# A four-layer convolution network in float32: second convolution's weights by accumulating transfers, shared rows copied, longer statistics pieces, one ScalarE reordering in the next chunk

## The chip, the core and the metric

The kernel runs on one core of a Trainium2 chip. A core has TensorE (PE, matrix products into PSUM), VectorE (DVE), ScalarE (ACT), GpSimd (POOL) and SyncE (SP), which work side by side, each in the order of its own queue, and wait for each other through semaphores. PEld is TensorE's loading of the stationary operand. Transfers are issued by SP, ACT or POOL and carried out by DMA engines. The metric is device time of one launch in microseconds (us); lower is better.

## The reference

The input `x` is (4, 256, 56, 56) in float32. Four layers follow each other, each `x = x + f(norm(x))`, where `norm` is a group norm over 8 channels and all positions. Layers 0 and 2 are involutions (a 7 x 7 kernel for each position, computed from the data), layer 3 gates by channel and position. The change lies in layer 1:

```
h = conv3x3(n, w1);  h = relu(bn1(h))        # n = norm(x)
h = conv3x3(h, w2);  h = bn2(h)
x = x + relu(n + h)
```

Each convolution has 256 channels in and out and a border of one zero.

## The kernel before, in words

`conv_layer` computes layer 1. Along a row, a 3-tap convolution is done for four outputs at a time with six products instead of twelve. A row of 56 becomes `WT` = 14 groups; `transform` makes six planes of the input (`v`, from the rows sorted into four phases, `ph1` or `ph2`); each of six planes of weights is multiplied with its plane on PE; and sums of the six results give the four outputs. The planes of weights from the three taps w0, w1, w2 of a row are: plane 0 6 w0, plane 1 w0 + w1 + w2, plane 2 w0 - w1 + w2, plane 3 w0 + 2 w1 + 4 w2, plane 4 w0 - 2 w1 + 4 w2, plane 5 24 w2. `row_weights` (L1236) makes them on DVE, for both convolutions, and `edge_weights` (L1265) scales planes 0 and 5 on ACT. PE takes the planes in the order 1, 2, 3, 4, 0, 5.

Channels lie on the 128 partitions, in two halves (`ci` of the input, `co` of the output). An image's rows are cut into three chunks, `C1_ROWS` for the first and `C2_ROWS` for the second convolution, so there are 12 chunks of each: (1, i) and (2, i). They are done in the order (1,0), (1,1), (2,0), (1,2), (2,1) and so on to (2,11): the second convolution runs one chunk behind. From chunk (1,1) on, the first convolution also saves products between pairs of rows (`columns`, `column_weights`, `filter_weights`), so a plane takes four products into two PSUM pairs, `inner` and `outer`; the second one (`unfiltered`) takes six products per half. PSUM holds four pairs, and a pair is reused when it has been read.

The order of all work is written out by hand. Each chunk has twelve slots, `after[0]` to `after[11]`; slot 2n runs inside the n-th plane of PE's order and slot 2n + 1 after its results were read. Other work is put there as small steps: loads, `phases` (L1322: the norm, and the sorting into phases, on ACT), `transform` (L1341, DVE) for the next chunk, and the weights at the start. `in_order` (L246) then ties each engine's instructions into program order, so a step that waits holds up all behind it on its engine.

At the end of a second convolution's chunk (`conv2`, L1506), `residual` (L1519, ACT) puts the normed input in `res`, `joined` (L1530, DVE) adds the convolution, ACT writes its relu in image order over the tile of x (L1542), and POOL issues a transfer that adds the layer's input to it (L1543) and one that stores it (L1544). `stats` (L1546) then sums pieces of 4 rows on DVE for layer 2's norm, in the next chunk's slots.

For layer 2, ten of these pieces of the last chunk are summed after the convolution has ended. Of the first convolution's chunk, the two outer output phases are written to `ph2` by `outputs` (L1432, ACT) in the next chunk, from the list `tail1`.

Of the kernel before, what the change touches and what calls it, by code (L numbers as in the profile page):

```python
# [56 lines left out]
C2_ROWS = [(0, 16), (16, 36), (36, 56)]  # L57
ST_ROWS = 4

# [12 lines left out]
def net_kernel(  # L72
# [1109 lines left out]
    def conv_layer(xin, xout, st, ahead):  # L1182
        with ExitStack() as es:
# [51 lines left out]

            def row_weights(u, wc, raw=None):  # L1236

                ws = []
                for ci in range(NB):
                    w = wc[ci * P : (ci + 1) * P].rearrange("c (y x) n -> c y x n", y=3)  # L1240
                    nc.sync.dma_start(u[:, ci, :, 0, :], w[:, :, 0, :])
                    nc.sync.dma_start(u[:, ci, :, 5, :], w[:, :, 2, :])
                    us = [u[:, ci, :, k, :] for k in range(WPOS)]
                    if raw is None:
                        w1 = new_xr()[:, : 3 * C].rearrange("p (y n) -> p y n", y=3)
                        nc.scalar.dma_start(w1, w[:, :, 1, :])
                        ws.append((us[0], w1, us[5], *us[1:5]))
                    else:
                        r = raw[ci][:, : 9 * C].rearrange("p (y x n) -> p x y n", y=3, x=3)
                        ws.append((r[:, 0], r[:, 1], r[:, 2], *us[1:5]))  # L1250
                yield
                for w0, w1, w2, u1, u2, u3, u4 in ws:
                    tt(u2, w0, w2, ALU.add)
                    tt(u1, u2, w1, ALU.add)
                    yield
                for w0, w1, w2, u1, u2, u3, u4 in ws:
                    tt(u2, u2, w1, ALU.subtract)
                yield
                for w0, w1, w2, u1, u2, u3, u4 in ws:
                    stt(u4, w2, 4.0, w0, ALU.mult, ALU.add)  # L1260
                    stt(u3, w1, 2.0, u4, ALU.mult, ALU.add)
                    stt(u4, w1, -2.0, u4, ALU.mult, ALU.add)
                    yield

            def edge_weights(u, ci):  # L1265

                for k, by in ((0, 6.0), (5, 24.0)):
                    nc.scalar.mul(u[:, ci, :, k, :], u[:, ci, :, k, :], by)

# [6 lines left out]
            def column_weights(ci, k0, k1):  # L1276

                w0, w1, w2 = (u1_sb[:, ci, y, k0:k1, :] for y in range(3))
                x = between_weights(ci, k0, k1)
                s = y_tile(3)[:, : (k1 - k0) * C].rearrange("p (k n) -> p k n", n=C)  # L1280
                tt(s, w0, w2, ALU.add)
                tt(x, s, w1, ALU.subtract)
                tt(w1, s, w1, ALU.add)
# [38 lines left out]
            def phases(i):  # L1322

                y0, y1, lo, hi = rows1(i)
                n, r0 = y1 - y0 + 2, lo - (y0 - 1)
                rstd, shift = norms[1][i // 3]
                if y0 == 0:
                    nc.vector.memset(ph1[:, :, 0], 0.0)
                if y1 == H:
                    nc.vector.memset(ph1[:, :, n - 1], 0.0)  # L1330
                for ci in range(NB):
                    at = ci * (CV_ROWS + 2) * W
                    xr = room["rows"][:, at : at + (hi - lo) * W].rearrange("p (r t j) -> p j r t", t=WT, j=4)
                    for j in range(4):
                        q, t0 = (j + 1) % 4, (j + 1) // 4
                        dst = ph1[:, PL[q], r0 : r0 + hi - lo, ci, t0 : t0 + WT]
                        s, t = rstd[:, ci : ci + 1], shift[:, ci : ci + 1]
                        nc.scalar.activation(dst, xr[:, j], AF.Identity, bias=t, scale=s)  # L1338
                        yield

            def transform(v, ph, y0, n):  # L1341

                rows = ph[:, :, y0 : y0 + n].rearrange("p j r c t -> p j (r c) t")
                at, size = rows[:, 0:1], ph.shape[2] * NB * (WT + 1)
# [33 lines left out]

            def new_v(key):
                v_of[key] = work.tile([P, WPOS, (CV_ROWS + 2) * NB, WT], F32, name="v")  # L1380
                return v_of[key]

            def input1(i):
                y0, y1, _, _ = rows1(i)
                n = y1 - y0 + 2
                yield from transform(new_v((1, i)), ph1, 0, n)

            def input2(i):
                y0, y1 = C2_ROWS[i % 3]
                yield from transform(new_v((2, i)), ph2, y0, y1 - y0 + 2)  # L1390

# [32 lines left out]
            def conv1(i, after, tail):  # L1424
# [4 lines left out]
                a, t, b, s, q = (y_tile(k)[:, : NB * n * WT] for k in (0, 1, 2, 5, 4))  # L1429
                home = {1: q, 2: s, 3: t, 4: s, 0: s}  # L1430

# [14 lines left out]
                for n_s, k in enumerate(KS):  # L1446
# [41 lines left out]
                    if k == 2:  # L1488
                        tt(full(a), full(q), got, ALU.add)
                        tt(full(q), got, full(q), ALU.subtract)  # L1490
                    elif k == 4:
# [14 lines left out]
            def conv2(i, after, sums, tail):  # L1506
# [23 lines left out]
                def joined(co):  # L1530
# [7 lines left out]
                    if i == n_chunks - 1:  # L1538
                        stt(xj, rj, 0.0, xj, ALU.max, ALU.add)
                        nc.sync.dma_start(xout[bb][co][:, at], x)  # L1540
                    else:
                        nc.scalar.activation(xj, rj, AF.Relu)  # L1542
                        nc.gpsimd.dma_start(x, xin[bb][co][:, at], accum_op=ALU.add)  # L1543
                        nc.gpsimd.dma_start(xout[bb][co][:, at], x)  # L1544

                def stats(co, ks):  # L1546

                    x = xr_of[i, co]
                    for k in ks:
                        at = (k * ST_ROWS - y0) * W  # L1550
                        nc.vector.bn_stats(sums[co][:, k, :], x[:, at : at + ST_ROWS * W])

# [36 lines left out]

                ks = list(range(y0 // ST_ROWS, y1 // ST_ROWS))  # L1590
                tail += [lambda co=co, part=part: stats(co, part) for co in range(NB) for part in (ks[:2], ks[2:])]


# [10 lines left out]
            order.append((2, n_chunks - 1))  # L1604
            late_v = None
            sums_of = {}


            since = mark()
            weights1, weights2 = row_weights(u1_sb, wc1, (room["h"], room["v2"])), row_weights(u2_sb, wc2)  # L1610
            next(weights1)
# [24 lines left out]
            for s, (conv, i) in enumerate(order):  # L1636
                after = [[] for _ in range(12)]
                for g in slow:
                    after[5].append(step(g))
                    after[11].append(step(g))  # L1640
                nxt = order[s + 1] if s + 1 < len(order) else None
                if conv == 1:
                    run_all(tail1)

                    if nxt[0] == 2:
                        j = nxt[1]
                        late_v = input2(j)
                        place(after, late_v, (1, 1, 3, 5, 8, 10))
                        if j == 0:
                            place(after, weights2, (3, 5, 7, 9, 11))  # L1650
                            for ci in range(NB):
# [6 lines left out]
                    else:  # L1658
                        j = nxt[1]
                        place(after, phases(j), [k // 2 for k in range(8)])  # L1660
                        after[3].append(lambda: load_rows(j + 1, xin))
                        place(after, input1(j), [4 + k // 2 for k in range(9)])
                        for ci in range(NB):
                            after[2 + ci].append(lambda ci=ci: edge_weights(u1_sb, ci))
                            after[4 + ci].append(lambda ci=ci: column_weights(ci, 1, 3))
# [3 lines left out]
                        for ci in range(NB):  # L1669
                            after[9 + ci].append(lambda ci=ci: column_weights(ci, 3, 5))  # L1670
                            after[10 + ci].append(lambda ci=ci: filter_weights(ci, 3, 5))
                        after[11].append(step(weights2))
                    conv1(i, after, tail1)
                else:
                    if i % 3 == 0:
                        sums_of[i // 3] = [
                            new_sums(H // ST_ROWS, work, 4)
                            if i // 3 < B - 1
                            else small.tile([P, H // ST_ROWS, 6], F32, name=f"st_c{co}", bufs=1)
                            for co in range(NB)  # L1680
# [3 lines left out]
                    tail1 = []  # L1684
                    if i == 0:
                        for ci in range(NB):
                            after[ci].append(lambda ci=ci: edge_weights(u2_sb, ci))
                    if late_v is not None:
                        place(after, late_v, (0, 0, 1))
                        late_v = None  # L1690
                    stats_at, loads_at = ((1, 2, 3, 4), (2, 4)) if i < n_chunks - 1 else ((3, 4, 6, 7), (4, 7))
                    for at, f in zip(stats_at, tail2):
                        after[at].append(f)
                    tail2 = []
# [20 lines left out]

            return tail2, sums_of[B - 1]

# [77 lines left out]
```

## Time and profile before

| what | us |
|---|---|
| median of 3 runs (1783.44 to 1788.03) | 1786.61 |
| profiled execution | 1782.26 |
| its span on the core | 1780.5 |
| PE busy | 1690.9 |
| DVE busy | 1359.5 |
| ACT busy | 904.5 |
| POOL busy | 398.2 |
| convolution layer, from its first product with weights to the next layer's first | 520.6 to 1228.6 |

The profile records one execution. A busy share is an average over stages: in the involution layers other things limit PE than in the convolution layer, so the layer concerned is read by itself. Behind a row of a timeline, the idle time before it stands in brackets with the engine and instruction that ended it. Names of lines (L1420) are those of the kernel before.

### The profile page before, as it was taken

Reading aid. Unit: us, or ns where it says so; the run is one execution under the profiler, and the core shown is the slowest. Engines: PE = TensorE matmul, PEld = TensorE weight load, DVE = VectorE, ACT = ScalarE, POOL = GpSimd, SP = SyncE. Lnnn points to the kernel's source line nnn. Section 1 sums busy time; section 2 is a strip of 40 time slices with the busy share of each in tenths; the row PEclk is TensorE's granted clock in tenths of the full one; section 3 lists DMA queues with packets and bytes.
Section 4 is the critical chain, followed back from the end, with each engine's and each line's share of the span. In section 5 each row is a group of like instructions: output and inputs, shape, how many; then the busy total and the mean of one; then the engine's idle time right before and its main releaser. Section 6 shows DMA issues by size and latency. Waiting matters only on the chain.

```text
span 1780.5 us, 55917 instructions
## 1 busy us (share of the span) xinstructions
PE 1690.9 (95%) x24216; PEld 1495.0 (84%) x24216; DVE 1359.5 (76%) x2529; ACT 904.5 (51%) x1926; POOL 398.2 (22%) x591
## 2 busy tenths in 40 slices
PE   6999999999998999999999999998999999899898
PEld 4998988889977988898889888986988888788786
DVE  2677787767779988789878887865877687677675
ACT  2655556555544334342344334223767567567564
POOL 2224321333210000000100000001000553563572
PEclk9999999999989999999999999999999999999996
DMA  2345443634652133331333232233445666665653
GB/s 86 125 162 169 139 151 135 198 108 130 207 173 80 41 87 77 94 75 51 90 92 76 52 87 55 63 126 108 144 142 164 188 210 193 209 208 162 187 152 115
DMA packets 71075, 227.46 MB, mean 128 GB/s; under 512 B 13141, under 2 KB 20830, under 8 KB 67118
## 3 DMA queue, kind: packets, MB, share of 16 engines
q1 hardware_dynamic: 55038, 160.97, 28.7%
q0 software_dynamic: 13952, 60.87, 12.1%
q8 instruction: 191, 3.13, 0.7%
q10 hardware_dynamic: 1840, 2.05, 0.4%
q14 instruction: 54, 0.44, 0.1%
HBM read 88.00 MB, written 49.15 MB: 77 GB/s over the span
## 4 chain that ended last, share of the span: by engine, by line
PE 57%; DVE 25%; ACT 7%; issue 5%; DMA 4%; POOL 1%; SPq 1%; ACTq 0%; DVEq 0%; POOLq 0%
PE mm L1420 18%; PE ps L592 14%; PE ps L634 13%; DVE kt L610 5%; PE ps L406 3%; DMA xw<-xw 3%; PE mm L1458 3%; DVE un L654 3%; ACT xs L1542 2%; PE ps L468 2%; DVE res L1534 1%; ACT res L1522 1%; DVE xs L1399 1%; DVE v L1362 1%; DVE st L1104 1%
## 5 line engine op out<-in xcount | busy, mean ns | idle before, releaser
L1420 PE MATMUL mm<-v,u_sb 128*128 128x280 f32 (+2 forms) x2136 | 478.0, 385 | 2.2 <-DVE v L1374 2.2
L1420 PEld LDWEIGHTS mm<-v,u_sb 128*128 128x128 f32 x2136 | 404.4, 190 | 71.4 <-issue 3.3
L634 PE MATMUL ps<-kt,xw 126*32 126x48 f32 (+1 forms) x12544 | 379.3, 235 | 19.4 <-DMA xw<-xw 7.4
L634 PEld LDWEIGHTS ps<-kt,xw 126*32 126x32 f32 (+1 forms) x12544 | 341.5, 122 | 64.4 <-issue 40.6
L592 PE MATMUL ps<-hp,z_sb 64*126 64x133 f32 x6144 | 383.7, 279 | 9.7 <-DVE kt L610 4.2
L592 PEld LDWEIGHTS ps<-hp,z_sb 64*126 64x126 f32 x6144 | 364.3, 186 | 25.4 <-DVE kt L610 6.4
L610 DVE TENSOR_TENSOR kt<-ps,zb_sb 126x798 f32<-126x798 f32 x352 | 332.9, 980 | 60.1 <-PE ps L592 59.6
L603 ACT ACTIVATE kt<-ps,zb_sb 126x133 f32<-126x133 f32 x960 | 280.2, 441 | 108.2 <-PE ps L592 108.2
L1458 PE MATMUL mm<-xs,u_sb 128*128 128x126 f32 (+1 forms) x1320 | 167.3, 280 | 19.1 <-DVE hp L1473 16.1
L1458 PEld LDWEIGHTS mm<-xs,u_sb 128*128 128x128 f32 x1320 | 159.4, 194 | 22.5 <-ACT ph L1338 16.1
L654 DVE SCALAR_TENSOR_TENSOR un<-ps,s,un 128x240 f32<-128x240 f32 x224 | 102.4, 457 | 90.7 <-ACT un L649 86.7
L654 DVE SCALAR_TENSOR_TENSOR un<-ps,par_sb,un 128x240 f32<-128x240 f32 x224 | 97.6, 456 | 82.3 <-ACT un L647 78.3
L418 ACT COPY xw<-ps 126x896 f32<-126x896 f32 x112 | 101.3, 906 | 50.2 <-PE ps L406 27.4
L406 PE MATMUL ps<-ident_sb,strip_sb 128*126 128x128 f32 x784 | 113.8, 285 | 13.5 <-issue 9.8
L659 POOL TENSOR_TENSOR xs<-un,xs 128x240 f32<-128x240 f32 x112 | 72.1, 664 | 216.9 <-DVE un L654 216.9
L149 POOL TENSOR_TENSOR norm_sb<-norm_sb,mhalf 128x1 f32<-128x1 f32 x32 | 19.3, 605 | 446.5 <-DVE norm_sb L148 446.5
L1543 POOL DMA_DIRECT2D xs<-x x22 | 19.7, 897 | 435.3 <-ACT xs L1542 435.3
L647 ACT ACTIVATE un<-ps,par_sb 128x240 f32<-128x240 f32 x112 | 50.1, 448 | 119.5 <-PE ps L634 110.7
L1542 ACT ACTIVATE xs<-res 128x1120 f32<-128x1120 f32 (+1 forms) x22 | 45.8, 2083 | 125.3 <-DVE res L1534 125.3
L406 PEld LDWEIGHTS ps<-ident_sb,strip_sb 128*126 128x126 f32 x784 | 85.6, 142 | 26.0 <-issue 11.8
L649 ACT ACTIVATE un<-ps,bn_t,s 128x240 f32<-128x240 f32 x112 | 60.1, 538 | 87.0 <-PE ps L634 80.0
L1338 ACT ACTIVATE ph<-xs,norm_sb 128x294 f32<-128x294 f32 (+2 forms) x96 | 82.0, 898 | 9.2 <-DMA xs<-x 7.5
(258 smaller groups left out, 1885.2 us busy)
## 6 DMA issues: line engine op xcount, KB each, us to landing
xw<-xw SPq DMA_DIRECT2D x224, 252.0 KB
xw<-xw SPq DMA_DIRECT2D x224, 126.0 KB
xs<-x SPq DMA_DIRECT2D x24, 560.0 KB
x<-xs POOLq DMA_DIRECT2D x8, 1568.0 KB, 8.1
xs<-x SPq DMA_DIRECT2D x8, 1568.0 KB
xs<-in_x_dram SPq DMA_DIRECT2D x6, 1568.0 KB
x<-xs SPq DMA_DIRECT2D x6, 1568.0 KB
gx<-x POOLq DMA_DIRECT2D x42, 224.0 KB, 5.2
```

The lines of the kernel that those rows point to most:

```text
L406: nc.tensor.transpose(ps[:Q, k * P : (k + 1) * P], flat[:, k * Q : (k + 1) * Q], ident_sb)
L418: nc.scalar.copy(xw[:, :NSB, :], ps[:Q, : NSB * P].rearrange("q (n c) -> q n c", n=NSB))
L592: nc.tensor.matmul(ps[:Q, i, k * NT : (k + 1) * NT], z_sb[i * R : (i + 1) * R, cb * GB // 2 + gp, z0 : z0 + Q], hp[i * R : (i + 1) * R, py ...
L603: nc.scalar.activation(kt[:, g0 + i, pb, :, k], ps[:Q, i, k * NT : (k + 1) * NT], AF.Identity, bias=zb_sb[:, cb * GB + g0 + i, p0 + k : p0 ...
L610: nc.vector.tensor_tensor(kt[:, g0 : g0 + 2, pb], ps[:Q, :, : PB * NT].rearrange("q i (k t) -> q i t k", k=PB), zb_sb[:, cb * GB + g0 : cb ...
L634: nc.tensor.matmul(v[m * j : m * j + m, i, :, k * TP : (k + 1) * TP], xw[:, window(ty), m * j : m * j + m], kt[:, ng * j : ng * j + ng, :, ...
L654: nc.vector.scalar_tensor_tensor(part, o[e], s, part, ALU.mult, ALU.add)
L659: nc.gpsimd.tensor_tensor(dst, u, dst, ALU.add)
L1338: nc.scalar.activation(dst, xr[:, j], AF.Identity, bias=t, scale=s)
L1420: nc.tensor.matmul(ps, *position(u, v, ci, dy, k, co, n), start=(j == 0), stop=(j == NB * 3 - 1))
L1458: nc.tensor.matmul(ps[:, bank, co * m : (co + 1) * m], u[ci][:, co * P : (co + 1) * P], v2[:, e, : n // 2, ci * WT : (ci + 1) * WT], start ...
L1542: nc.scalar.activation(xj, rj, AF.Relu)
```

## The change

Five edits are made together.

1. `summed_weights` replaces `row_weights` for the second convolution. The taps are loaded straight into the planes, ACT scales what needs a factor, and POOL issues nine steps of two transfers (one for each half `ci`) which add further taps from HBM, or plane 5, to what stands in a plane. Its last step is the scaling of planes 0 and 5, which was at the start of chunk (2,0) before and is now in slot 11 of (1,1).
2. `phases` and `transform` leave out the first two rows of a chunk that is not an image's first. ACT copies them, in all six planes, from the chunk before (`nc.scalar.copy` in `transform`). The planes stand in two fixed tiles, `v0` and `v1`, instead of tiles that rotate; the first convolution uses `v1` (chunk 0: `v0`), the second `v0` (last chunk: `v1`).
3. `stats` sums pieces of up to 8 rows (`ST_ROWS`), so a chunk of 20 rows has pieces of 8, 8 and 4.
4. ACT's reordering (L1542) and POOL's two transfers of the second half become `added`, and for `co` = 1 run in slot 0 of the next chunk (`late_x`).
5. `outputs` at the end of chunk (1,0) moves into slot 0 of (1,1); plane 1's result of a chunk then goes to another buffer, `first`. `transform` for the second convolution has five steps, not six, in the first convolution's slots.

The diff, cut to its core:

```diff
-ST_ROWS = 4
+ST_ROWS = 8
+ST_PIECES = [-(-(y1 - y0) // ST_ROWS) for y0, y1 in C2_ROWS]
...
+            def summed_weights(u, wc):
+
+                cis = range(NB)
+                w = [wc[ci * P : (ci + 1) * P].rearrange("c (y x) n -> c x y n", y=3) for ci in cis]
+                us = [[u[:, ci, :, k, :] for k in range(WPOS)] for ci in cis]
+                w1 = [new_xr()[:, : 3 * C].rearrange("p (y n) -> p y n", y=3) for ci in cis]
+                for ci in cis:
+                    nc.sync.dma_start(w1[ci], w[ci][:, 1])
+                    nc.sync.dma_start(us[ci][5], w[ci][:, 2])
+                    for k in (0, 1, 3):
+                        nc.sync.dma_start(us[ci][k], w[ci][:, 0])
+                yield
+                for ci in cis:
+                    nc.scalar.mul(us[ci][2], w1[ci], -1.0)
+                    nc.scalar.mul(us[ci][4], w1[ci], -2.0)
+                    nc.scalar.mul(us[ci][5], us[ci][5], 4.0)
+                    yield
+                for k, x in ((1, 1), (2, 0), (1, 2), (2, 2), (3, 1), (4, 0), (3, 1), (4, None), (3, None)):
+                    for ci in cis:
+                        by = us[ci][5] if x is None else w[ci][:, x]
+                        nc.gpsimd.dma_start(us[ci][k], by, accum_op=ALU.add)
+                    yield
+                for ci in cis:
+                    for k in (0, 5):
+                        nc.scalar.mul(us[ci][k], us[ci][k], 6.0)
+                yield
...
-                n, r0 = y1 - y0 + 2, lo - (y0 - 1)
+                n, r0, known = y1 - y0 + 2, lo - (y0 - 1), 2 if i % 3 else 0
...
-                    xr = room["rows"][:, at : at + (hi - lo) * W].rearrange("p (r t j) -> p j r t", t=WT, j=4)
+                    xr = room["rows"][:, at + known * W : at + (hi - lo) * W].rearrange("p (r t j) -> p j r t", t=WT, j=4)
...
-            def transform(v, ph, y0, n):
-
+            def transform(v, ph, y0, n, known):
+
+                if known is not None:
+                    old, m = known
+                    nc.scalar.copy(
+                        v[:, :, : 2 * NB].rearrange("p k r t -> p k (r t)"),
+                        old[:, :, m * NB : (m + 2) * NB].rearrange("p k r t -> p k (r t)"),
+                    )
+                    v, y0, n = v[:, :, 2 * NB :], y0 + 2, n - 2
...
+            v_sb = [wpool.tile([P, WPOS, (CV_ROWS + 2) * NB, WT], F32, name=f"v{k}") for k in range(2)]
...
+                first = y_tile(3)[:, : NB * n * WT] if i else q
+                home = {1: first, 2: s, 3: t, 4: s, 0: s}
...
-                        nc.scalar.activation(xj, rj, AF.Relu)
-                        nc.gpsimd.dma_start(x, xin[bb][co][:, at], accum_op=ALU.add)
-                        nc.gpsimd.dma_start(xout[bb][co][:, at], x)
...
+                        late_x.append(lambda: added(x, xj, rj, co, at))
+                        if co == 0:
+                            run_all(late_x)
+
+                def added(x, xj, rj, co, at):
+
+                    nc.scalar.activation(xj, rj, AF.Relu)
+                    nc.gpsimd.dma_start(x, xin[bb][co][:, at], accum_op=ALU.add)
+                    nc.gpsimd.dma_start(xout[bb][co][:, at], x)
+
+                def stats(co, k):
+
+                    r0, r1 = k * ST_ROWS, min(n, (k + 1) * ST_ROWS)
+                    at = sum(ST_PIECES[: i % 3]) + k
+                    nc.vector.bn_stats(sums[co][:, at, :], xr_of[i, co][:, r0 * W : r1 * W])
...
+                after[0] += late_x
+                late_x.clear()
                 if conv == 1:
-                    run_all(tail1)
+                    after[0] += tail1
+                    tail1 = []
...
-                        place(after, late_v, (1, 1, 3, 5, 8, 10))
+                        place(after, late_v, (1, 1, 3, 5, 8))
                         if j == 0:
-                            place(after, weights2, (3, 5, 7, 9, 11))
+                            place(after, weights2, (0, 1, 2, 11))
...
+                        place(after, weights2, (0, 4, 5, 5, 6, 7, 8, 9, 10))
                         place(after, input1(j), [4 + k // 2 for k in range(9)])
...
-                    if i == 0:
-                        for ci in range(NB):
-                            after[ci].append(lambda ci=ci: edge_weights(u2_sb, ci))
                     if late_v is not None:
-                        place(after, late_v, (0, 0, 1))
+                        place(after, late_v, (0, 0, 1, 1))
...
```

## The prediction

> **What bounds the kernel now.** I read the page's totals and slices first, then the chain that ended last, then busy time by stretch, TensorE's waits, and the timelines around the longest ones. The page:
>
> ```profile
> span 1780.5 us, 55917 instructions
> ...
> PE   6999999999998999999999999998999999899898
> ...
> PE 57%; DVE 25%; ACT 7%; issue 5%; DMA 4%; POOL 1%; SPq 1%; ACTq 0%; DVEq 0%; POOLq 0%
> ```
>
> TensorE (PE) is busy nearly everywhere. The change touches only the convolution layer, 515.8 to 1230.5 us, so what can be won is PE's idle time there. The stretches (columns: stretch, length, busy time of PE, PEld, DVE, ACT, POOL, then clock, DMA share, GB/s):
>
> ```profile
> 545.00:600.00 55.00, 45.49 (x280) 41.78 (x279) 51.22 (x88) 25.04 (x46) 0.00 (x0) 0.97 0.17 49
> 620.00:1230.50 610.50, 598.16 (x3462) 533.18 (x3462) 507.64 (x907) 224.55 (x268) 35.81 (x50) 1.00 0.30 80
> ```
>
> PE idles 9.5 us in 545 to 600, where VectorE (DVE) is 93% busy, and 12.3 us in the rest of the layer. Shorter stretches show the granted clock at 0.66 in 575 to 580 and 0.67 in 600 to 605, after those gaps: another 1.7 us lost in each. Who PE waited for, in the layer:
>
> ```profile
> PE mm L1458 <- DVE hp L1473: 16.1, 13, 2.8
> PE mm L1420 <- DVE v L1374: 2.2, 1, 2.2
> ```
>
> Nearly all is a PSUM pair that DVE has not yet read (L1473), and one late plane of the transformed input (L1374). DVE before that plane, from its timeline:
>
> ```profile
> 594.93 0.95 DVE L1260 SCALAR_TENSOR_TENSOR u_sb<-u_sb 128x768 f32<-128x768 f32 x1
> 595.91 0.96 DVE L1261 SCALAR_TENSOR_TENSOR u_sb<-xs,u_sb 128x768 f32<-128x768 f32 x1
> 596.91 0.96 DVE L1262 SCALAR_TENSOR_TENSOR u_sb<-xs,u_sb 128x768 f32<-128x768 f32 x1
> 597.78 1.20 DVE L1372 SCALAR_TENSOR_TENSOR v<-v 128x1008 f32<-128x1008 f32 x1
> 599.02 0.68 DVE L1374 SCALAR_TENSOR_TENSOR v<-v 128x504 f32<-128x504 f32 x1
> ```
>
> The second convolution's weights stand in DVE's order ahead of the plane PE needs at 599.85. A later gap, from the timelines of ACT, DVE and PE:
>
> ```profile
> 680.46 2.24 ACT L1542 ACTIVATE xs<-res 128x1120 f32<-128x1120 f32 x1 [1.45 <-DVE res L1534]
> 682.50 0.44 ACT L1468 COPY xs<-mm 128x280 f32<-128x280 f32 x1
> 682.97 0.45 DVE L1472 TENSOR_TENSOR hp<-xs,mm 128x280 f32<-128x280 f32 x1 [1.89 <-ACT xs L1468]
> 693.45 1.19 PE L1458 MATMUL mm<-xs,u_sb 128*128 128x140 f32 x8 [0.72 <-DVE hp L1473]
> ```
>
> ScalarE (ACT) ends a chunk with a 2.24 us reordering; the next chunk's first PSUM copy stands behind it, DVE loses 1.89 us, and PE pays 0.72 us some 10 us later.
>
> **The Trainium skill.** "DMA: Bandwidth & Descriptors", section "SWDGE vs HWDGE vs iDMA", ties accumulating transfers to GpSimd; the trace agrees: L1543 is the only accumulating line and is POOL's. Its "Rules for kernel authors" say an accumulate reads its destination and writes it later, so one into the same bytes must wait for the former's semaphore; here L1544 waits for L1543 (118.2 us in 22). Its "Issuing engines are not separate DMA queues" says that all queues share 16 engines, which I use for the loads in between. "TensorE: Matmul & The Clock Gate", "What's actually happening": an idle window of about 3.4 us halves the clock; 0.66 and 0.67 above agree, though after shorter gaps in a row.
>
> **The change part by part.**
>
> *Weights, DVE side.* Twelve operations go: 2 x (0.95 + 0.96) at L1253/L1254, 2 x 0.95 at L1257, 2 x (0.95 + 0.96 + 0.96) at L1260 to L1262: 11.5 us of DVE, all inside 572 to 598. `outputs` of the first chunk also moves behind ACT's first copy of chunk (1,1); that copy came at 561.82 because 2.15 us of `outputs` preceded it, so DVE starts 2 us sooner. Adding up DVE's remaining operations of (1,1) in order (five rounds of 1.5 us, 6.9 of combinations, 3.7 of `columns`, 3.8 of `transform`, 2.6 of `column_weights`, 0.8 of norm) from 558.7, I find PE waiting about 0.7 and 1.1 us, ending (1,1) at 555.0 + 24.1 + 1.8 = 581, and planes 1 and 2 of conv2(0) by 590. DVE alone would have plane 3 by 588, so it no longer sets this.
>
> *Weights, the transfers.* ACT gains six scalings (826 ns each, L1268's row), 5.0 us where it is half idle; SP gets ten loads; POOL gets eighteen accumulating transfers of 384 KB in rows of 1 KB. Rows in the trace's DMA records: accumulating, 3584 B take 291 ns and 4480 B 356; plain loads of these sizes 140 and 173, so twice that plus 10; a plain 1 KB row takes 46. An accumulated 1 KB row is then 102 ns by this extension, and with 24 rows on each of 16 engines a transfer is 2.5 us. No run shows one: at the long rows' byte rate it would be 2.0 us, at 291 ns whatever the length 7.0. I take 2.5.
>
> Start: phases(1)'s rows land by 525; the weight loads follow in SP's queue at 1.4 us each (four took about 6.4 us with row loads beside them in 535 to 543), so the ninth, which POOL's second transfer needs, lands near 541. POOL is in order and waits for nothing else that is late: an issue costs 0.9 us for 128 rows (L1543), perhaps 1.7 for 384, less than 2.5, and a transfer into the same plane always has three others between. Last landing: 541 + 1.5 (issue) + 17 x 2.5 + about 6 (four loads of `rows`, 1.3 us of every engine each, and a weight load) + 1 = 592.
>
> *What waits for it.* The four scalings of planes 0 and 5 now stand at the end of (1,1) on ACT and wait for that landing, since the last accumulation reads plane 5. Behind them: 0.8 for the last scaling, two L1437 at 0.55, the new copy of shared rows (0.45 by L1468's 280 columns). DVE's first `transform` step of chunk (1,2) overwrites rows this copy reads, so it waits, and plane 3 of conv2(0) stands behind it: three operations of 0.65. Together 4.6 us with handovers: PE's third plane starts at 597 instead of 599.85, gain 2.7. If the landing comes before 585 all this is hidden and PE itself sets 590. One long gap in place of several leaves one clock loss of two: gain 1.7.
>
> *Shared rows.* Sixteen chunks transform two rows less: six operations of one plane lose 0.06 us (798 against 734 ns for 56 columns), three of two planes 0.12: 0.7 us per chunk of DVE. Sixteen ACT copies of 0.45 pay for it, and 64 `phases` operations shorten by about 0.03 to 0.05. The copy is a new wait of DVE on ACT: in conv1 slots it comes behind the moved reordering (2.24), and DVE stalls perhaps 0.5 us. Cost on PE nothing, since the DVE start gained below is larger.
>
> *The reordering.* L1468 no longer stands behind L1542: DVE starts 1.9 us sooner in each chunk. Gaps after 620 from PE's timeline: 0.39, then seven single ones (0.72, 0.73, 0.48, 0.71, 0.48, 0.72, 0.41) vanish: 4.6. Two chunks have several (2.14, 0.29, 1.14; 2.15, 1.45): there DVE needs 5.6 us per plane against PE's 3.8, so only 1.9 each is won: 3.8. Gain 8.4. POOL's accumulate and store of the second half start some 2 us later; the statistics that wait for them run a chunk later, so nothing.
>
> *Statistics.* 112 of 379 ns become 48 of 620 (L1104's 448 columns) and 16 of 379: 6.6 us of DVE where it waits for PE anyway. At the layer's end ten pieces become six: 0.2.
>
> Sum: 2.7 + 1.7 + 8.4 + 0.2 = 13.0. The profiled execution took 1782.3 (span 1780.5), giving 1769.3; the median of the runs is 4.3 higher, so 1773.6 is predicted.
>
> **Rivals.** *Transfers in time.* At 2.0 us each the last lands near 584: gain 9.8 at plane 3, both clock losses 3.4, and 8.6: 1764.8. For it: accumulation may simply follow bytes. Against: the 10 ns per row above, and the engines near full throughout.
>
> *Transfers too slow (the other side).* POOL's accumulations set the end of conv2(0)'s wait. They cancel all other gains when the last lands at about 605, 3.2 us each, 135 ns per row; slower by 0.3% from 612. At 200 ns per row (4.8 us) it lands at 632, PE starts plane 3 at 636, 36 later, against 10 won: 1812. For it: no 1 KB accumulation was seen, and fixed costs per row would be paid 6,912 times. Against: the two sizes seen extend to 102.
>
> *The gaps stay.* The change does not do what it says after 620, because DVE now waits for ACT's copy behind the reordering: only 4.4 won, 1782.2. For it: ACT then does 2.24 + 0.45 ahead of DVE's step. Against: DVE needs 1.6 of that for itself.
>
> **How the numbers follow.** Under 0.3% (5.4 us) a measurement of this kernel can't be told from no change. Chances: forecast 0.44 (own range 1766 to 1780), in time 0.22, gaps stay 0.12, landing between 601 and 612 (about no change) 0.06, too slow 0.16. Faster is 0.44 + 0.22, same 0.12 + 0.06, slower 0.16. From 1762 to 1789 holds all but the slow case and a little of the others.
>
> **What would show it.** Right: no L1253 to L1262 on DVE for the second convolution; accumulations of about 2.5 us each, the last landing near 592; ACT's scaling and then PE's third plane waiting for it around 597; single gaps gone after 620. Wrong: an accumulated row far from 102 ns, PE waiting at planes 1 or 2, or gaps after 620 above 5 us in sum.

## The result, and the profile after

| | before | after |
|---|---|---|
| median of the runs, us | 1786.61 (1783.44 to 1789.93) | 1761.49 (1759.64 to 1766.93) |
| profiled execution, us | 1782.26 | 1761.49 |
| its span, us | 1780.5 | 1759.7 |

The ratio is 0.9862 with a 95% interval of 0.984 to 0.9884. The kernel after is 25.1 us faster by the medians and 20.8 us by the two profiled executions, so it gained more than the 13.0 forecast, and ended 4.5 us below the forecast's own range of 1766 to 1780, and 0.5 below the wide one of 1762 to 1789. From the page of the kernel after:

```profile
span 1759.7 us, 55922 instructions
...
PE   6999999999999999999999999998999999989998
...
PE 71%; DVE 13%; DMA 5%; ACT 4%; issue 3%; SPq 1%; POOL 1%; ACTq 0%; DVEq 0%; POOLq 0%
```

In the slices of PE the 8 in the convolution layer's first part is gone, and the chain that ended last runs through PE for 71% instead of 57%. The stretches (columns as before: stretch, length, busy time of PE, PEld, DVE, ACT, POOL, then clock, DMA share, GB/s):

```profile
545.00:600.00 55.00, 51.70 (x323) 48.22 (x322) 51.80 (x94) 27.35 (x50) 17.18 (x15) 1.00 0.84 155
575.00:580.00 5.00, 5.00 (x41) 4.86 (x40) 4.83 (x11) 2.59 (x6) 0.00 (x0) 1.00 1.18 197
600.00:605.00 5.00, 5.00 (x28) 5.00 (x27) 2.69 (x6) 0.22 (x1) 0.00 (x0) 1.00 0.00 0
...
620.00:1208.00 588.00, 583.78 (x3371) 521.22 (x3370) 486.17 (x845) 221.02 (x274) 33.67 (x47) 1.00 0.30 81
```

PE idles 3.3 us in 545 to 600 instead of 9.5, and the clock is full where it was 0.66 and 0.67. In the rest of the layer PE idles 4.2 us instead of 12.3. PE's waits in the layer (who waits, for whom, us in total, times, longest):

```profile
PE mm L1492 <- DVE hp L1507: 3.3, 6, 1.0
...
PE mm L1492 <- DVE xs L1507: 1.4, 2, 0.7
...
PE mm L1492 <- ACT xs L1502: 1.2, 1, 1.2
PE mm L1492 <- DVE hp L1509: 1.1, 1, 1.1
```

L1507 is L1473 of before: 16.1 us in 13 waits have become 3.3 in 6, and the wait for a plane of `v` doesn't appear at all. Chunk (2,0), from the timelines of PE, ACT and DVE:

```profile
583.80 27.49 PE L1453 MATMUL mm<-v,u_sb 128*128 128x224 f32 x144
580.49 3.02 ACT L1285 ACTIVATE u_sb<-u_sb 128x768 f32<-128x768 f32 x4
584.40 0.45 ACT L1368 COPY v<-v 128x336 f32<-128x336 f32 x1
588.73 0.68 DVE L1404 SCALAR_TENSOR_TENSOR v<-v 128x504 f32<-128x504 f32 x1
```

All 144 products of the chunk run without a break; the third plane, complete with DVE's L1404 at 589.4, is reached at 593.0. The four last scalings (L1285) have no bracket: ACT was busy until then, and the last accumulation, which by the records of the transfers landed at 580.6, kept nobody waiting. A later chunk's end, from the timelines of ACT and DVE:

```profile
671.20 2.29 ACT L1582 ACTIVATE xs<-res 128x1120 f32<-128x1120 f32 x1 [0.65 <-DVE res L1568]
673.27 0.49 ACT L1368 COPY v<-v 128x336 f32<-128x336 f32 x1
671.73 0.44 DVE L1506 TENSOR_TENSOR hp<-xs,mm 128x280 f32<-128x280 f32 x1
673.79 1.39 DVE L1392 SCALAR_TENSOR_TENSOR v<-ph 128x560 f32<-128x560 f32 x2 [0.42 <-ACT v L1368]
```

DVE's L1506 (L1472 of before, where it lost 1.89 us) starts without a wait. The new copy of shared rows does stand behind the reordering, and costs DVE 0.42 us.

Three lengths are used from here on, all from PE's timeline: the *first stage* from the first product of chunk (1,1) to that of (1,2), and the *rest* from there to the next layer's first product. Each is from one profiled execution. The chunk before, (1,0), takes 34.0 to 34.8 us by the clock at its start, whatever was changed, and is left out. Kernels which don't differ in a stage agree in it within 0.05 us, but for the rest of before and of only_weights, where the clock is lost at different places. Each ratio is to executions of before that were taken beside it; their medians were 1784.66 to 1786.61.

| | first stage | rest | median | ratio to before (95%) |
|---|---|---|---|---|
| before | 64.79 | 608.26 | | |
| after | 54.81 | 596.85 | 1761.49 | 0.9862 (0.984 to 0.9884) |
| no_weights | 63.52 | 596.83 | 1771.68 | 0.9922 (0.9896 to 0.9948) |
| no_late | 54.80 | 607.23 | 1774.06 | 0.9936 (0.9913 to 0.996) |
| no_rows | 55.03 | 596.17 | 1763.85 | 0.9871 (0.9846 to 0.9897) |
| st4 | 54.81 | 596.85 | 1763.82 | 0.9881 (0.9857 to 0.9905) |
| only_weights | 57.22 | 609.92 | 1779.98 | 0.9966 (0.9949 to 0.9984) |
| only_late | 64.80 | 596.39 | 1773.13 | 0.9935 (0.9911 to 0.996) |
| extra2 | 54.82 | 596.80 | 1762.35 | 0.9873 (0.9846 to 0.9899) |
| extra9 | 84.13 | 596.81 | 1791.8 | 1.0038 (1.0017 to 1.006) |
| no_tail | 56.87 | 596.85 | 1766.2 | 0.9889 (0.9874 to 0.9904) |
| held6 | 81.30 | 596.84 | 1791.08 | 1.0032 (1.0019 to 1.0044) |
| norms_conv2 | 53.40 | 601.28 | 1766.47 | 0.9896 (0.9878 to 0.9915) |
| norms_early | 53.37 | 591.73 | 1756.39 | 0.9839 (0.9808 to 0.9871) |

### The profile page after: what moved, and what is told of

It is laid out like the page before. It is cut to its first block, busy times and chain, and to the rows that moved or that the text cites. A ratio compares the mean times of both kernels' runs of the same rounds, so it can differ in the third digit from the quotient of the medians.

```text
span 1759.7 us, 55922 instructions
## 1 busy us (share of the span) xinstructions
PE 1687.6 (96%) x24216; PEld 1494.0 (85%) x24216; DVE 1338.6 (76%) x2469; ACT 912.6 (52%) x1948; POOL 417.5 (24%) x609
## 3 DMA queue, kind: packets, MB, share of 16 engines
q10 hardware_dynamic: 1040, 1.26, 0.3%
## 4 chain that ended last, share of the span: by engine, by line
PE 71%; DVE 13%; DMA 5%; ACT 4%; issue 3%; SPq 1%; POOL 1%; ACTq 0%; DVEq 0%; POOLq 0%
PE mm L1453 24%; PE ps L635 14%; PE ps L593 14%; PE mm L1492 9%; DVE kt L611 5%; PE ps L407 3%; DMA xw<-xw 3%; DVE un L655 3%; PE ps L469 2%; DMA u_sb<-in_wc_dram 1%; DVE st L1105 1%; ACT hp L488 1%; ACT xw L419 1%; PE ps L718 1%; PE ps L947 1%
## 5 line engine op out<-in xcount | busy, mean ns | idle before, releaser
L1492 PE MATMUL mm<-xs,u_sb 128*128 128x126 f32 (+1 forms) x1320 | 163.0, 277 | 7.0 <-DVE hp L1507 3.3
```

The costliest lines, as they stand in the source:

```text
L1492: nc.tensor.matmul(ps[:, bank, co * m : (co + 1) * m], u[ci][:, co * P : (co + 1) * P], v2[:, e, : n // 2, ci * WT : (ci + 1) * WT], start ...
```

## The experiments

The theory (A) says that each of two edits removes one cause: the accumulated weights take DVE's operations out of the first stage, the moved reordering takes ACT's delay out of the rest, and shared rows and longer pieces are worth nothing. The rival (B) says that DVE's load as a whole decides, so that every edit which relieves DVE gains in proportion, wherever it stands.

**One edit undone.** *no_weights* makes the second convolution's weights on DVE again (the old slots and ACT's scalings in chunk (2,0) come back with it):

```diff
...
-            weights1, weights2 = row_weights(u1_sb, wc1, (room["h"], room["v2"])), summed_weights(u2_sb, wc2)
+            weights1, weights2 = row_weights(u1_sb, wc1, (room["h"], room["v2"])), row_weights(u2_sb, wc2)
...
```

> The changed kernel with the second convolution's weights made on VectorE again (edit 1 undone, all else kept). Theory A, each edit removes one cause (the weights the gaps of the start, about 10 us; the moved reordering the gaps after it, about 11 us; shared rows and statistics nothing): ratio to the kernel before about 0.992, some 10 us above the changed kernel, TensorE's third plane of chunk (2,0) waiting again for VectorE. Rival B, VectorE's load as a whole decides, and shared rows and statistics relieve it: the start is mended in part by them, so only 3 to 5 us are lost, ratio 0.988 to 0.989.

It loses 8.7 us in the first stage and nothing in the rest. The third plane waits again, 3.35 us for DVE's step of `transform`, at 597.59.

*no_late* runs the reordering and POOL's transfers at the chunk's end again:

```diff
-                        late_x.append(lambda: added(x, xj, rj, co, at))
-                        if co == 0:
-                            run_all(late_x)
+                        added(x, xj, rj, co, at)
```

> The changed kernel with ScalarE's reordering of the second half at its old place (edit 4 undone). Theory A: the gaps after the start come back, 10 to 11 us lost, ratio about 0.992. Rival B: VectorE has 0.7 us per chunk less to do and makes up for the late start, so only 2 to 4 us are lost, ratio 0.987 to 0.988.

It loses 10.4 us in the rest, and nothing in the first stage. The gaps of the rest come back from 4.2 to 9.6 us, and the clock is lost at both image starts (0.91 in 840 to 860, 0.96 in 1000 to 1040), some 3.4 us; about 1 us of the loss is not accounted for.

*no_rows* transforms all rows of a chunk again:

```diff
-                n, r0, known = y1 - y0 + 2, lo - (y0 - 1), 2 if i % 3 else 0
+                n, r0, known = y1 - y0 + 2, lo - (y0 - 1), 0
...
-                known = (v_of[1, i - 1], p1 - p0) if i % 3 else None
+                known = None
...
-                known = (v_of[2, i - 1], p1 - p0) if i % 3 else None
+                known = None
```

> The changed kernel with every chunk transforming all its rows (shared rows not copied, the fixed tiles kept). Theory A: 0 to 2 us slower, ratio 0.986 to 0.987. Rival B: the gaps after the start come back in part, 5 to 8 us slower, ratio 0.989 to 0.991.

Without shared rows the rest is 0.7 us shorter and the first stage 0.2 longer, though DVE has more to do. The second gap at each image start is 0.29 us without ACT's copy and 0.67 or 0.69 with it, so by the stages shared rows cost PE half a us in all. The intervals of the ratios don't separate the two kernels.

*st4* sums pieces of 4 rows again:

```diff
-ST_ROWS = 8
+ST_ROWS = 4
```

> The changed kernel with statistics over pieces of 4 rows again. Theory A: 0 to 0.5 us slower, ratio 0.986. Rival B: 1 to 3 us slower, ratio 0.987 to 0.988.

Both stages are as after: nothing. Theory A stands and B falls: less load of DVE alone won nothing here, and without the one or the other of A's two edits 8.7 and 10.4 us are lost, each in its own stage.

**One edit alone.** *only_weights* is the kernel before with `summed_weights` in its slots; its diff from before, without the new function:

```diff
-            weights1, weights2 = row_weights(u1_sb, wc1, (room["h"], room["v2"])), row_weights(u2_sb, wc2)
+            weights1, weights2 = row_weights(u1_sb, wc1, (room["h"], room["v2"])), summed_weights(u2_sb, wc2)
...
-                            place(after, weights2, (3, 5, 7, 9, 11))
+                            place(after, weights2, (0, 1, 2, 11))
...
+                        place(after, weights2, (0, 4, 5, 5, 6, 7, 8, 9, 10))
...
-                        after[11].append(step(weights2))
...
-                    if i == 0:
-                        for ci in range(NB):
-                            after[ci].append(lambda ci=ci: edge_weights(u2_sb, ci))
```

> The kernel before with the second convolution's weights by accumulating transfers alone (edit 1). Theory A: about 10 us faster, ratio 0.994, the gaps after the start as before. Rival B: less, 4 to 6 us, because VectorE stays loaded by whole rows: ratio 0.997.

*only_late* is the kernel before with the reordering moved:

```diff
-                        nc.scalar.activation(xj, rj, AF.Relu)
-                        nc.gpsimd.dma_start(x, xin[bb][co][:, at], accum_op=ALU.add)
-                        nc.gpsimd.dma_start(xout[bb][co][:, at], x)
+                        late_x.append(lambda: added(x, xj, rj, co, at))
+                        if co == 0:
+                            run_all(late_x)
...
+                after[0] += late_x
+                late_x.clear()
```

> The kernel before with the second half's reordering, accumulation and store in slot 0 of the next chunk alone (edit 4). Theory A: 10 to 11 us faster, ratio 0.994; single gaps after 620 gone, the start as before. Rival B: 2 to 4 us faster, ratio 0.998.

The reordering alone gains 11.9 us in the rest, and nothing in the first stage. The weights alone gain 7.6 in the first stage. Their rest is 1.7 longer than before, with gaps of about the same sum (12.6 against 12.4): the clock is lost at one image start more. So the ratio, 0.9966, is the one that rival B named and not A's 0.994: A was 2.4 us too high for the first stage, and had no place for the clock. B's reason for it, that whole rows keep DVE loaded, doesn't fit no_rows; no_tail below finds most of the 2.4. From PE's timeline at the same gap, first of before, then of only_weights:

```profile
852.78 1.19 PE L1458 MATMUL mm<-xs,u_sb 128*128 128x140 f32 x8 [2.14 <-DVE hp L1473]
```

```profile
847.61 1.80 PE L1485 MATMUL mm<-xs,u_sb 128*128 128x140 f32 x8 [2.12 <-DVE hp L1500]
```

After gaps of nearly one length the same eight products take 1.19 us in one and 1.80 in the other (the clock is 1.00 and 0.91 in 840 to 860), so the length of such a gap doesn't decide whether it costs the clock too. What the kernel after has over the weights alone in the first stage, 2.4 us, should then lie in the fifth edit.

**The move of `outputs`.** *no_tail* undoes that part alone; the order of the other engines is untouched:

```diff
-                    after[0] += tail1
+                    run_all(tail1)
                     tail1 = []
```

> The kernel after with outputs at the end of chunk (1,0) run ahead of slot 0 of (1,1) again, so that ACT writes the two outer output phases (some 2.2 us) before its first PSUM copy of (1,1). Nothing else is changed. Theory A: DVE starts (1,1) 2 us later, a PE gap of about 2.2 us comes at 565, and chunk (1,2) starts about 3 us later than in the kernel after, which is the difference between the kernel after (10.5 us won by then) and the weights alone (7.5); time 1763.5 to 1765.5. If the move is worth nothing, the start stays within 0.5 us and the missing 3 us lie in another edit.

From the timelines of ACT and PE:

```profile
560.86 2.15 ACT L1471 ACTIVATE ph<-hp,bn_t,s 128x280 f32<-128x280 f32 x4
562.92 0.35 ACT L1502 COPY xs<-mm 128x252 f32<-128x252 f32 x1
564.19 2.02 PE L1492 MATMUL mm<-xs,u_sb 128*128 128x126 f32 x16 [2.24 <-DVE hp L1507]
```

The first copy of the chunk stands behind 2.15 us of `outputs` again, and PE pays 2.24 at once. The first stage loses 2.06 us. With only_weights' 7.57 that makes 9.63 of the 9.98 won in it.

**How much later could the transfers land?** *extra2* and *extra9* add 4 and 18 accumulations behind the last one, into planes 3 and 4 (so these planes' weights aren't the reference's); below is extra2's:

```diff
+                for k, x in ((3, 0), (4, 0),):
+                    for ci in cis:
+                        nc.gpsimd.dma_start(us[ci][k], w[ci][:, x], accum_op=ALU.add)
                 for ci in cis:
                     for k in (0, 5):
```

> The changed kernel with two more steps (four transfers) that add a tap once more to planes 3 and 4, so the second convolution's weights are not the reference's. At 2.0 us each the last landing moves from 580.6 to about 589. If the third plane of chunk (2,0) can wait until the landing plus 4.6 us, it starts near 593.5 against 592.8: within 1 us of the changed kernel. If the transfers were already at the edge of the path, 6 to 8 us slower.

> The changed kernel with nine more steps (eighteen transfers), weights again not the reference's. Last landing about 617, then 4.6 us by ScalarE's scaling, its copy of shared rows and VectorE: TensorE's third plane of chunk (2,0) starts near 621.5, 29 us late, with one loss of the clock: ratio about 1.002. If only the plane's own landing counts and nothing stands behind ScalarE's scaling, 24 to 25 us: ratio 0.999 to 1.000.

Four more change nothing: those into plane 3 landed at 587.5 and 589.5, ahead of the 593.0 at which PE takes it, and the last one, into plane 4, at 594.7 instead of the 589 expected. Eighteen more land at 617.6, the first half of plane 3 at 615.3, and PE waits for that:

```profile
616.06 21.42 PE L1456 MATMUL mm<-v,u_sb 128*128 128x224 f32 x96 [26.06 <-DMA u_sb<-in_wc_dram]
```

The wait is 26.06 us. The 96 products that follow take 21.25 us from their start to that of (1,2), where the kernel after has 18.16. That is slower than the kernel before. The wait is near the 24 to 25 us of the second case, and the stage still loses the 29 us of the first, as the clock takes 3.1 more. PE waits here for the landing itself, since ACT's scalings don't depend on what was added. So *held6* puts twelve ahead of the step that adds plane 5 to plane 4, and thus ahead of the scalings (planes 3 and 4 again aren't the reference's):

```diff
+                    if (k, x) == (4, None):
+                        for extra in (3, 4) * 3:
+                            for ci in cis:
+                                nc.gpsimd.dma_start(us[ci][extra], w[ci][:, 0], accum_op=ALU.add)
                     for ci in cis:
                         by = us[ci][5] if x is None else w[ci][:, x]
```

> The kernel after with twelve more accumulating transfers of 384 KB (planes 3 and 4, three times each and half, from the first tap) ahead of the one that adds plane 5 to plane 4, so the weights of these planes are not the reference's. At the 2.02 us per transfer seen, the last lands at 580.6 + 12 x 2.02 = 605, and ACT's last scalings, which the last accumulations hold, wait for it. Theory A (the prediction's chain behind the landing: scalings, copy of shared rows, three operations of DVE, 4.6 us): PE's third plane starts at about 609.6 and chunk (1,2) some 20 us later than in the kernel after; about the time of the kernel before, 1781 to 1787. Rival (the chain is hidden, as PE waits for the landing alone): third plane at about 605, time 1776 to 1781.

The last lands at 610.1, not at 605: the added ones take some 2.7 us each, as POOL waits for the former one into the same plane (up to 4.8 us at once) and loads of rows run beside them. From the timelines of ACT, DVE and PE:

```profile
610.51 0.84 ACT L1289 ACTIVATE u_sb<-u_sb 128x768 f32<-128x768 f32 x1 [0.66 <-DMA u_sb<-u_sb]
612.24 0.45 ACT L1372 COPY v<-v 128x336 f32<-128x336 f32 x1
612.72 1.28 DVE L1396 SCALAR_TENSOR_TENSOR v<-ph 128x504 f32<-128x504 f32 x2 [27.34 <-ACT v L1372]
614.69 20.86 PE L1457 MATMUL mm<-v,u_sb 128*128 128x224 f32 x96 [23.80 <-DVE v L1408]
```

The chain is as the prediction described it: the last scaling, `outputs`, the copy of shared rows, DVE, PE. From the landing to PE's third plane it takes 614.69 - 610.1 = 4.6 us, and the kernel is 0.3% slower than before.

**What is left of the gaps.** After the change, gaps remain in (1,1) and in two chunks where an image starts, 839 to 849 and 1008 to 1018. In all of these a norm holds a PSUM pair, from a product in slot 11 of one chunk to DVE's reading in slot 5 of the next. Theory A2 says that this makes the gaps; B2 says that DVE is simply behind there. *norms_conv2*:

```diff
-                for g in slow:
-                    after[5].append(step(g))
-                    after[11].append(step(g))
+                if conv == 2:
+                    for g in slow:
+                        place(after, g, (1, 4, 5, 8, 9, 11))
```

> The kernel after, with the steps of layer 1's own norm (norm_steps for an image) placed only in the second convolution's chunks, in slots 1, 4, 5, 8, 9 and 11, instead of in slots 5 and 11 of every chunk. Theory A2 (what is left of PE's gaps comes from the norm holding a PSUM pair from slot 11 of one chunk to slot 5 of the next, so that the first convolution, which needs two pairs per plane, has too few): the 3.3 us of gaps before chunk (1,2) and the 3.7 us at the two image starts (839 to 849, 1008 to 1018) mostly go, and the time falls by 3 to 6 us below the kernel after, ratio 0.983 to 0.985. Rival B2 (in these chunks DVE is simply behind, 5.6 us per plane against PE's 3.8): the gaps stay within 1 us in sum, and the ratio stays at 0.986.

The first stage gains 1.4 us: of its four gaps, 3.3 us in sum, those of 0.19 and 1.11 go. A2 expected most of the 3.3; the gaps of 1.21 and 0.79 stay, so a held pair doesn't make them, and their cause stays open. The rest is 4.4 us longer. From the timelines of POOL, DVE and PE:

```profile
842.14 0.56 POOL L1584 DMA_DIRECT2D x<-xs  x1 [5.24 <-DMA xs<-x]
842.71 1.08 POOL L150 TENSOR_TENSOR norm_sb<-norm_sb,mhalf 128x1 f32<-128x1 f32 x2
843.32 0.16 DVE L233 SCALAR_TENSOR_TENSOR norm_sb<-gm,norm_sb 128x1 f32<-128x1 f32 x1 [3.70 <-POOL norm_sb L150]
845.50 1.19 PE L1492 MATMUL mm<-xs,u_sb 128*128 128x140 f32 x8 [1.20 <-DVE hp L1507]
```

POOL's step of the norm now stands behind the store of the chunk's first half, which waits 5.24 us for its accumulation. DVE's last step of the norm waits 3.70 for POOL, and PE 1.20 for DVE. The pair had been free long before, but this new wait hides what that brought. *norms_early* puts POOL's step ahead of the transfers (the edit against norms_conv2):

```diff
-                        place(after, g, (1, 4, 5, 8, 9, 11))
+                        place(after, g, (1, 2, 3, 5, 7, 11))
```

> As the run before with the norms only in the second convolution's chunks, but in slots 1, 2, 3, 5, 7 and 11, so that POOL's operation of the norm (L150) stands ahead of POOL's transfers of the first half instead of behind them. Theory A2 (a held PSUM pair makes the gaps; in the run before, DVE's last norm step waited 3.7 to 4.3 us for POOL, which stood behind the transfer of the chunk's first half, and this made new gaps): no DVE wait for L150 over 1 us, the gaps at the image starts below 0.5 us each, those before chunk (1,2) 2.0 as in the run before; layer about 685.8 - 1.3 - 3.3 = 681.2, time 1755 to 1758, ratio 0.982 to 0.985. Rival B2 (DVE is behind in the image-start chunks whatever holds the pair): gaps of 1.5 to 2 us in each of the two image-start chunks stay, layer 684 to 685.

PE's waits in its layer, and the timelines of POOL and PE at the same place:

```profile
PE mm L1492 <- ACT xs L1502: 1.2, 1, 1.2
...
PE mm L1492 <- DVE hp L1507: 0.8, 1, 0.8
```

```profile
824.62 1.57 POOL L150 TENSOR_TENSOR norm_sb<-norm_sb,mhalf 128x1 f32<-128x1 f32 x2 [35.57 <-DVE norm_sb L149]
842.24 3.02 PE L1492 MATMUL mm<-xs,u_sb 128*128 128x140 f32 x24
846.05 3.02 PE L1492 MATMUL mm<-xs,u_sb 128*128 128x140 f32 x24
```

Between the first stage and the layer's end no gap is left. DVE's first sum of the image-start chunk, in the kernel after and here:

```profile
838.00 0.44 DVE L1506 TENSOR_TENSOR hp<-xs,mm 128x280 f32<-128x280 f32 x1
```

```profile
836.52 0.44 DVE L1506 TENSOR_TENSOR hp<-xs,mm 128x280 f32<-128x280 f32 x1
```

PE began the chunk at 834.68 and 832.70, so DVE is 3.3 us behind it in the one and 3.8 in the other. The layer is 6.6 us shorter than after's, the median 1756.39, a ratio of 0.9839 (0.9808 to 0.9871): the fastest kernel of the study by its median, though its interval overlaps that of the kernel after; that it is faster rests on the stages, 53.37 and 591.73. B2 falls: DVE runs the same operations up to the last of the old gaps (here 0.2 us of the norm more), starts them later, and with a fourth pair PE waits for none of them.

## Why the prediction was wrong

**The step that failed: "24 rows on each of 16 engines a transfer is 2.5 us."** The row itself was right. In the records of the transfers of the kernel after, 6,912 accumulated rows of 1 KB have a median of 102 ns, which is the forecast. Multiplying it by 24 was wrong, because rows of one engine overlap. The transfers of the kernel after in 545 to 575 (kind of queue: packets, MB, share of 16 engines' time):

```profile
q0 software_dynamic: 5604, 5.51, 116.3%
```

A share over 100% means more than one row in an engine at a time. The transfers were completed every 2.01 us for most of the way (547.21, 549.22, 551.23, 553.25), 384 KB at some 195 GB/s; 24 x 102 ns in 2.01 us are a share of 1.22, which is what the short stretches show (1.23, 1.23, 1.24 between 545 and 565). "DMA: Bandwidth & Descriptors" of the Trainium skill, section "Two DMAs through the same engine are not ordered", says that descriptors of one engine start in order but are pipelined, with reading and writing apart; the trace agrees on the overlap (116%) and doesn't show the two sides, and I hadn't taken that into the sum. The prediction's other value, 2.0 us from the long rows' byte rate, agrees with the 2.01 measured.

What followed from it: POOL's second transfer was issued at 540.0 (forecast 541), the seventeen intervals took 37.5 us instead of 42.5 and about 6 for loads, and the last landed at 580.6 instead of 592. Where I had put 6 us for loads in between, two intervals are longer than the others, by 1.7 and 1.3 us. With that, ACT's scalings waited for nothing, and the case called *transfers in time* came. Its mechanism was right, but the fit of its sum is luck: 9.8 + 3.4 + 8.6 = 21.8, where the two profiled executions differ by 20.8 and their layers by 21.9, is 3.2 us too much in the first stage (13.2 against 9.98) and 2.8 too little behind it (8.6 against 11.4).

**The chain behind the landing** (4.6 us) was right, but idle in the kernel after; held6 shows it to a tenth. So was the place where all is cancelled: "about 605", and slower by 0.3% from 612 (605 and 5.4 us make 610.4); held6 landed at 610.1, and its ratio is 1.0032. The slower side was a matter of some twelve transfers ahead of the scalings.

**The first stage.** Forecast 2.7 + 1.7, measured 9.98. PE took up the third plane 44.87 us after the stage's start in the kernel before and takes it up after 36.66 now, 8.2 us sooner; the 96 products from there on took 19.92 us and take 18.16, 1.8 less. The products behind two gaps of before, and behind the one at 573 now:

```profile
576.05 4.52 PE L1458 MATMUL mm<-xs,u_sb 128*128 128x126 f32 x24 [2.77 <-DVE hp L1473]
599.85 20.08 PE L1420 MATMUL mm<-v,u_sb 128*128 128x224 f32 x96 [2.19 <-DVE v L1374]
```

```profile
573.12 2.91 PE L1492 MATMUL mm<-xs,u_sb 128*128 128x126 f32 x24 [0.79 <-DVE hp L1507]
```

Idle time in the stage fell from 9.52 to 3.30 us, 6.2. The lost clock, for which I kept one loss of two, was won back twice: 1.6 in the 24 products (4.52 before, 2.91 after) and the 1.8 in the 96. The prediction's sum is wrong here too: the loss at 576 lies ahead of the third plane, so it is already inside the 2.7 and inside the rival's 9.8, and I added it once more. PE's waits in (1,1) were forecast at 1.8 and are 3.3 in four gaps; two of these, 0.19 and 1.11, go when no norm holds a pair. The move of `outputs` was listed with its 2.15 us, and no_tail shows 2.06 of it on PE.

**The reordering.** Forecast 8.4, measured 11.4 in the rest. The mechanism and the idle time were right: gaps fell from 12.35 to 4.23, 8.1 us; the single ones are all gone, and the image starts kept 1.83 and 1.86 of some 3.6 each, so about 1.7 was won in each where 1.9 was forecast. What is missing is two terms that I left out. First, before lost the clock once in the rest, 0.91 in 1020 to 1040, after the gap of 2.15 at an image start: 20 x 0.09 = 1.8 us. This part is not sure to come, since the gap of 2.14 at 852.78 in the same execution cost no clock. Nor did it take the idle window of about 3.4 us that the prediction goes by: the gap of 2.15 stood alone, with none listed in the 47 us before it. Second, a gap costs more than its idle time. In the kernel after, 24 products take 2.86 us where nothing intervenes (850.65 to 853.51), and 3.30, 3.77 and 4.06 with a gap of 0.20, 0.67 and 0.96 among them (from 836.67, 840.92 and 845.64), so each gap costs 0.24 more than its idle time. "TensorE: Matmul & The Clock Gate" of the Trainium skill, section "Step-by-step: what each phase is for", says that the drain of one product is covered by the next in a stream, and that a product which stands alone can't hide it; 0.24 us per gap (products and their weight loads together) fits that, though no run here shows what the 0.24 consist of. Seven gaps fewer make 1.7, and 8.1 + 1.8 + 1.7 = 11.6. The same sum fits norms_early: six gaps with 3.69 us of idle time and 6 x 0.24 make 5.13, and its rest is 5.12 shorter. My price for the image starts was nearly right, but its reason, that DVE needs 5.6 us per plane there, was not enough: norms_early has no gap with the same DVE work.

**Shared rows and statistics**, forecast at nothing in PE's stages, are within 0.7 us of it. DVE's stall on the copy was forecast at 0.5 and is 0.42. The 0.2 of the statistics at the layer's end lies behind the two stages, and the medians don't resolve it.

**The median.** I added 4.3 us, by which the median of before lay above its profiled execution. After's profiled execution is its median, so this difference did not carry over; it belonged to the one execution that was profiled. It made even the right rival 3.3 us too high (1764.8 against 1761.49).

## What to carry to other kernels

The duration of a transfer's row is not the time it takes up in its engine: rows overlap, so take a queue's throughput from completed bytes per time, and look for a share above 1. Work out how late a hidden transfer may land and what chain stands behind it, and try it with a few transfers more: here four behind the last one were free, and twelve ahead of the scalings undid the whole change. A gap of TensorE costs its idle time and something more, 0.24 us here, and where a buffer is held by a side task such as a norm, moving that task can be worth as much as making the busy engine faster, if none of its steps lands behind a waiting transfer.

## What the runs showed of the hardware

Accumulating transfers of 384 KB in 1 KB rows ran at 2.0 us each and 195 GB/s with 16 engines, at a share of up to 1.24; POOL needed 1.13 to 1.27 us to issue one. After PE's waits of 23.8 and 26.06 us the next 96 products took 20.69 and 21.25 us from start to start instead of 18.16, so the clock came back only after a loss of 2.5 and 3.1 us, more than the 1.6 and 1.8 us after gaps of 2.77 and 2.19. In one execution a lone gap of 2.15 us cost the clock and one of 2.14 us did not.
